# Attention with an adapter: two small transposes move into the free quarters of the score banks, and ahead in TensorE's order

## The chip, the core and the metric

The kernel runs on one core of one Trainium2 chip. The metric is the device time of one execution in microseconds. A profiled execution has a span of its own, from its first to its last instruction, and a time, which is a little longer. PE is TensorE, DVE is VectorE, ACT is ScalarE, POOL is GpSimd, SP is SyncE. PSUM is the memory that PE writes; it has eight banks, each of 512 fp32 columns in 128 partitions.

## The reference, cut to what matters

Four blocks follow one another on x of shape (4, 256, 512): attention with an adapter, a gated FFN, a state-space mixer (most of the time), the gated FFN again. The change is in the first.

```python
B, T, C = x.shape            # 4, 256, 512; 32 heads of 16
qkv = einsum('btc,oc->bto', layernorm(x), w_attn)
q, k, v = split(qkv, 3)      # each (B, 32, T, 16)
q, k = rope(q), rope(k)
scores = where(causal, einsum('bhqd,bhkd->bhqk', q, k) / sqrt(16), -inf)
y = einsum('bhqk,bhkd->bhqd', softmax(scores), v)
# ten adapter tokens: keys ak and values av from w_attn
ascores = gating[0] * softmax(einsum('bhqd,xhkd->bhqk', q, ak) / sqrt(512))
y = y + einsum('bhqk,xhkd->bhqd', ascores, av)
x = x + einsum('btc,oc->bto', y, w_proj)
x = x + ffn(layernorm(x))    # then the mixer, then the FFN again
```

## The kernel before, in words

All of attention is the function `attention`. It has three PSUM pools. `ps` ("a_m") is a ring of three banks for nearly everything: projections (`pq`), turned stacks (`trp`), turned weights (`ptr`), adapter scores (`pa`), and small transposes. `ps_s` ("a_s") has four banks for the scores, each holding 3 x 128 of its 4 x 128 columns. `ps_y` ("a_y") has one for the weighted values `py`.

The prologue prepares batch 0: it splits the weights into upper and lower parts, normalizes x, makes two products each for q and k and two for v (12 matmuls each, `mm3`, lines L115 to L117), and rotates q and k (`rotated`: three DVE instructions from PSUM at L323, L326 and L327, one POOL sum at L329). `stacked` (L342, L343, on POOL) and `pieces` (transposes at L444, a copy at L447, a DMA `pc` on SP's queue) turn them into the form that the scores need. In the prologue a scheduler orders the instructions of every engine.

Then comes a loop of 32 steps: batch b, and u, one of eight groups of four heads. In it PE's order is the program's order (a manual schedule for TensorE alone), while the scheduler orders the other engines. The order of a step i on PE is:

1. the 16 score matmuls of (b, u) at L492; on even steps behind the first `adapter_scores` (`pa`, L457, copied to `sa`, L462); the transposes of `pieces` (L444). DVE reduces the scores in eight instructions (L500), which also write them masked to SBUF; ACT takes exponentials (L508).
2. the "long" item of the step: a product for the next batch's q, k or v (12 matmuls), for an output projection `po`, or for the FFN `pd`; steps 8, 16, 24, 26 and 27 have none. Then "values" items (`pya`).
3. `weigh(i-2)`, 16 matmuls into `py` (L533, L539), which DVE copies to `ys` in `taken` (L547).
4. `turn(i-1)`: 12 transposes into three `ptr` (L523), copied to `eT` by ACT, DVE and ACT (L524).
5. `gathered(i-3)`: two transposes of `ys` into `try` (L553), a DVE reciprocal (L558) and product `y` (L559).
6. the asides: on even steps the second half of `adapter_scores`, two transposes into `tra` (L466) that ACT copies to `as` (L467).
7. "turn" items: `tr` (the normalized x, L166), `pt` (adapter weights, L584), the closing `try2` (L610).

`gathered` and the asides before take a bank each from the three-bank ring, as `ptr` does.

Of the kernel before, what the change touches and what calls it, by code (L numbers as in the profile page):

```python
# [9 lines left out]
F32 = mybir.dt.float32  # L10
# [10 lines left out]
P = 128  # L21
B, L, C = 4, 256, 512
# [4 lines left out]
NH, HD = 32, 16  # L27
# [52 lines left out]
def hybrid_kernel(  # L80
# [18 lines left out]
    a_s = keep.tile([P, 1], F32, name="a_s")  # L99
# [172 lines left out]
    def attention(later, region):  # L272
        with ExitStack() as es:
# [5 lines left out]
            p3 = pool("a3", 3)  # L279
            ps, ps_s, ps_y = (  # L280
                banks.enter_context(tc.tile_pool(name=name, bufs=bufs, space=PSUM))
                for name, bufs in (("a_m", 3), ("a_s", 4), ("a_y", 1))
            )

            acon = w1.tile([P, NCOL_ATTN - NCOL_KEEP], F32, name="acon")
            col = lambda name: acon[:, COLS[name][0] - NCOL_KEEP : COLS[name][1] - NCOL_KEEP]
            rot = col("rot").rearrange("p (c f s d) -> p c f s d", c=2, f=2, s=2)
# [20 lines left out]
                return xs  # L308

            def projected(xs, w, where):  # L310
                pq = where[0].tile([P, C], F32, name="pq", tag=where[1])
                mm3(pq, [[v[:, k, :] for v in xs] for k in range(KC)],
                    [[v[:, k, :] for v in w] for k in range(KC)])
                return pq

            def rotated(pq, c, f, name):

                pv = pq.rearrange("p (h d) -> p h d", h=NH)
                cos, sin = (
                    rot[:, c, f, s, :].unsqueeze(1).to_broadcast([P, NH, HD]) for s in range(2)  # L320
                )
                t1 = p2.tile([P, NH, HD], F32, name="t1", tag="t1")
                nc.vector.tensor_tensor(t1, pv, cos, ALU.mult)  # L323
                t2 = p1.tile([P, NH, HD], F32, name="t2", tag="t2")
                hd = HD // 2
                nc.vector.tensor_tensor(t2[:, :, :hd], pv[:, :, hd:], sin[:, :, :hd], ALU.mult)  # L326
                nc.vector.tensor_tensor(t2[:, :, hd:], pv[:, :, :hd], sin[:, :, hd:], ALU.mult)  # L327
                r = p2.tile([P, NH, HD], F32, name=name, tag=name)
                nc.gpsimd.tensor_tensor(r, t1, t2, ALU.add)  # L329
                return r  # L330
# [23 lines left out]
            AW = 8 * NA  # L354
# [50 lines left out]

            def prepared(b):

                where = (ps, "m") if b else (ps_s, "sc")
                r = {0: -6, 1: 1}.get(b, 8 * (b - 1))
                xs = []  # L410

                def made(c, f):
                    w = wk_s if f else wq_s
                    qk[b, c, f] = rotated(projected(xs[c], w, where), c, f, f"r{f}{c}")

                yield "turn", r
                xs.append(normed(norm, 2 * b))
                yield "long", r + 1
                made(0, 0)
                yield "turn", r + 1  # L420
                xs.append(normed(norm, 2 * b + 1))
                yield "long", r + 2
                made(0, 1)
                yield "long", r + 3
                made(1, 0)
                yield "long", r + 4
                made(1, 1)
                where = (ps, "m")
                for c in range(2):
                    yield "long", r + 5 + c  # L430
                    nc.scalar.copy(
                        values(vs[b % 2], c)[:, :, :HD],
                        projected(xs[c], wv_s, where).rearrange("p (h d) -> p h d", h=NH),
                    )

            def pieces(b, q, f):
# [16 lines left out]
            def adapter_scores(b, q):  # L453
                pa = ps.tile([AW, L], F32, name="pa", tag="m")
                for j in range(4):
                    n = (4 * q + j) * AW
                    nc.tensor.matmul(  # L457
                        pa, akbd[:, n : n + AW], turned_[b, q][0][:, 0, j % 2, :],
                        start=(j == 0), stop=(j == 3),
                    )  # L460
                sa = p2.tile([AW, 4, P], F32, name="sa", tag="paT").rearrange("p s i -> p (s i)")[:, :L]
                nc.scalar.copy(sa, pa)  # L462
                yield
                tr = ps.tile([P, 2, AW], F32, name="tra", tag="m")
                for c in range(2):
                    nc.tensor.transpose(tr[:, c, :], sa[:, c * P : (c + 1) * P], ident[:AW, :AW])  # L466
                nc.scalar.copy(  # L467
                    state[b]["as"][:, :, q * 8 : q * 8 + 8, :].rearrange("p c h a -> p c (h a)"), tr
                )
# [11 lines left out]
            def scores(b, u):  # L481

                qT, kT = turned_[b, u // 2]
                es_ = [p2.tile([P, 4, (c + 1) * P], F32, name=f"e{c}", tag=f"e{c}") for c in range(2)]
                tops = {}
                banks_ = [ps_s.tile([P, 3, P], F32, name="sc", tag="sc") for _ in range(4)]
                for c, at in ((1, slice(0, 2)), (0, slice(2, 3))):
                    n = (c + 1) * P
                    for v in range(2):
                        for r in range(4):  # L490
                            rows = slice(32 * r, 32 * r + 32)
                            nc.tensor.matmul(  # L492
                                banks_[r][:, at, :].rearrange("p k i -> p (k i)"),
                                qT[rows, 0, u % 2, c * P : (c + 1) * P], kT[rows, v, u % 2, :n],
                                start=(v == 0), stop=(v == 1),
                            )
                for c, at in ((1, slice(0, 2)), (0, slice(2, 3))):
                    tops[c] = nm = p3.tile([P, 4], F32, name="nmx", tag="nmx", bufs=4)
                    for r in range(4):
                        nc.vector.tensor_tensor_reduce(  # L500
                            es_[c][:, r, :].rearrange("p (k i) -> p k i", i=P), banks_[r][:, at, :],
                            mask[:, 1 - c :, :], -1.0, 3e38, ALU.add, ALU.min, nm[:, r : r + 1],
                        )

                yield
                for c in (1, 0):
                    for r in range(4):
                        nc.scalar.activation(  # L508
                            es_[c][:, r, :], es_[c][:, r, :], AF.Exp, scale=-1.0, bias=tops[c][:, r : r + 1],
                        )  # L510
                    if c == 0:
                        all_es[8 * b + u] = es_
                    yield
# [34 lines left out]
                return ys  # L548

            def gathered(b, u, ys):  # L550
                tr = ps.tile([P, 2, 4, 32], F32, name="try", tag="m")
                for c in range(2):
                    nc.tensor.transpose(  # L553
                        tr[:, c].rearrange("p h d -> p (h d)"), ys[:, c * P : (c + 1) * P], ident
                    )
                st = state[b]
                ry = p2.tile([P, 2, 4], F32, name="ry")
                nc.vector.reciprocal(ry, tr[:, :, :, HD])  # L558
                nc.vector.tensor_tensor(  # L559
                    st["y"][:, :, 64 * u : 64 * u + 64].rearrange("p c (h d) -> p c h d", h=4),  # L560
                    tr[:, :, :, :HD], ry.unsqueeze(3).to_broadcast([P, 2, 4, HD]), ALU.mult,
                )
# [73 lines left out]
            def fed(f, t):  # L636
# [12 lines left out]
            wq_s, wk_s, wv_s = (  # L649
                [wpool.tile([P, KC, C], F32R, name=f"{v}{j}") for j in range(2)] for v in ("wq", "wk", "wv")  # L650
            )
# [25 lines left out]
            all_es, eTs, yss = {}, {}, {}  # L677
            feed = None
            asides, nexts = [], {}
# [10 lines left out]
            def step(stage, i):  # L690

                for j in [j for j, (s, r) in nexts.items() if s == stage and r <= i]:
                    moved(j, i)
# [15 lines left out]
            with tc.manual_schedule(engines={nc.tensor.engine}):  # L709
                for i in range(n):  # L710
                    b, u = divmod(i, 8)
# [20 lines left out]
                    next(scoring)  # L732
                    step("long", i)
                    step("values", i)
                    if 2 <= i:
                        py = weigh(*divmod(i - 2, 8), eTs.pop(i - 2))
                    if 1 <= i:
# [1 line left out]
                    next(scoring)  # L739
                    if 2 <= i:  # L740
                        yss[i - 2] = taken(py)
                    if 3 <= i:
                        gathered(*divmod(i - 3, 8), yss.pop(i - 3))
                    while asides:
                        next(asides.pop(0), 0)
                    step("turn", i)
                    if u == 7:
                        moved(adapted(b), i)
# [6 lines left out]
                    b, u = divmod(i + 3, 8)  # L755
# [17 lines left out]
                b = B - 1  # L773
# [26 lines left out]
            ps = ctx.enter_context(tc.tile_pool(name="m_m", bufs=2, space=PSUM, **freed))  # L800
# [1111 lines left out]
```

## Time and profile before

| | us |
|---|---|
| three runs | 1806.4, 1806.55, 1808.31 (median 1806.55) |
| profiled execution, its time | 1805.61 |
| its span | 1803.8 |
| mean granted clock of TensorE | 0.989 |
| the loop's first scores | 31.71 |
| PE busy from 135 to 180 us | 42.81 of 45 |
| PE, DVE, ACT, POOL busy over the span | 97%, 79%, 70%, 13% |

The loop of 32 steps and its end take the stretch from 31.71 us to about 290; at about 315 us the mixer is under way and takes nearly all the rest. A step with a long product takes 6.5 to 10 us, one without 4.7 to 8.7. Busy shares are means over stages, so the stretches matter more than the totals. A row of the trace's timeline has the start, the duration, the engine, the line and the tiles; in brackets stands idle time before it and what ended it. Matmuls overlap in the pipeline, so that a row's duration can reach into the next row.

### The profile page before, as it was taken

The page shows a single profiled execution, that of the slowest core. Times are in us where ns is not written, and L with a number is a line of the kernel's source. Part 1 is how long each engine was busy: PE and PEld are TensorE (multiplying, and loading weights), DVE is VectorE, ACT ScalarE, POOL GpSimd, SP SyncE. Part 2 cuts the span into 40 slices and gives each one's busy share as a digit, 9 for nine tenths or more (in the row PEclk, how much of TensorE's full clock was granted, in tenths as well). Part 3 has the DMA queues.
Part 4 walks back from the last instruction along what each step waited for, and adds up shares of the span by engine and source line. Part 5 has one row for each costly group of instructions (what it writes and reads, how often), then busy time and mean ns, then how long its engine had stood idle before and what let it go on. Part 6 is the DMA issues. An engine that isn't in the chain of part 4 may idle for free.

```text
span 1803.8 us, 33220 instructions
## 1 busy us (share of the span) xinstructions
PE 1745.7 (97%) x12862; PEld 1417.8 (79%) x12862; DVE 1427.7 (79%) x2523; ACT 1268.7 (70%) x2293; POOL 240.9 (13%) x249
## 2 busy tenths in 40 slices
PE   7999988899999999999999999999999999999998
PEld 6777767778877888888888888888888888888877
DVE  5676676889998788787878797878788878887777
ACT  5676684578887668766866686668667867777754
POOL 5332320111110111011110101110111101101100
PEclk8999999999999999999999999999999999999999
DMA  4000100122344234423433252325333433343231
GB/s 157 19 19 19 47 26 26 43 71 99 109 127 137 80 106 154 120 85 99 153 100 100 88 162 90 109 81 176 103 94 112 135 106 94 115 138 115 85 97 56
DMA packets 136941, 173.71 MB, mean 96 GB/s; under 512 B 12752, under 2 KB 78032, under 8 KB 136784
## 3 DMA queue, kind: packets, MB, share of 16 engines
q1 hardware_dynamic: 127712, 138.57, 25.5%
q10 hardware_dynamic: 9072, 33.03, 4.8%
q8 instruction: 101, 1.65, 0.4%
q14 instruction: 56, 0.46, 0.1%
HBM read 131.71 MB, written 35.65 MB: 93 GB/s over the span
## 4 chain that ended last, share of the span: by engine, by line
PE 76%; DVE 11%; ACT 8%; issue 3%; DMA 1%; POOL 1%; SPq 0%; ACTq 0%; DVEq 0%; POOLq 0%
PE pp L115 13%; PE pp L117 12%; PE pp L116 12%; PE pyy L1252 7%; PE pog L115 6%; PE pog L117 6%; PE pog L116 6%; PE trx L1233 3%; DVE acc L980 2%; ACT e L508 1%; ACT em L1213 1%; DVE em L1226 1%; PE pq L115 1%; PE ptr L523 1%; PE pq L117 1%
## 5 line engine op out<-in xcount | busy, mean ns | idle before, releaser
L115 PE MATMUL pp<-mx,w 128*128 128x512 f32 x1144 | 459.3, 401 | 0.0
L117 PE MATMUL pp<-mx,w 128*128 128x512 f32 x1144 | 446.8, 391 | 0.0
L116 PE MATMUL pp<-mx,w 128*128 128x512 f32 x1144 | 446.1, 390 | 0.0
L1285 POOL TENSOR_TENSOR sq<-sq,x 128x1024 f32<-128x1024 f32 x54 | 132.1, 2446 | 1177.7 <-ACT x L1284 1177.7
L117 PEld LDWEIGHTS pp<-mx,w 128*128 128x128 f32 x1144 | 214.7, 188 | 46.2
L115 PEld LDWEIGHTS pp<-mx,w 128*128 128x128 f32 x1144 | 214.8, 188 | 44.7
L980 DVE SCALAR_TENSOR_TENSOR acc<-pp,cw_s,acc 128x1012 f32<-128x1012 f32 (+2 forms) x192 | 244.5, 1274 | 4.3
L116 PEld LDWEIGHTS pp<-mx,w 128*128 128x128 f32 x1144 | 215.1, 188 | 40.5
L1226 DVE TENSOR_TENSOR em<-em,gm 128x1280 f32<-128x1280 f32 x128 | 189.5, 1489 | 72.1 <-ACT em L1221 72.1
L115 PE MATMUL pog<-wo,gh 128*128 128x512 f32 x512 | 201.2, 393 | 2.0 <-DVE x L1381 2.0
L117 PE MATMUL pog<-wo,gh 128*128 128x512 f32 x512 | 200.2, 391 | 0.9 <-DVE gh L1364 0.9
L116 PE MATMUL pog<-wo,gh 128*128 128x512 f32 x512 | 199.8, 390 | 0.0
L1236 DVE TENSOR_TENSOR xd<-trx,dt_t 128x512 f32<-128x512 f32 x128 | 82.4, 685 | 141.5 <-PE trx L1233 141.5
L1152 ACT ACT_TABLE_LOAD x63 | 80.8, 1283 | 139.1 <-DVE acc L980 138.9
L1443 ACT ACTIVATE gt<-pp 128x1024 f32<-128x1024 f32 x64 | 65.6, 1025 | 145.0 <-PE pp L117 145.0
L1252 PEld LDWEIGHTS pyy<-em,xd 64*64 64x64 f32 x4096 | 130.2, 133 | 44.2 <-issue 17.6
L1213 ACT ACTIVATE em<-r,end_t 128x128 f32<-128x128 f32 x512 | 163.1, 389 | 0.8
L1252 PE MATMUL pyy<-em,xd 64*64 64x256 f32 (+3 forms) x4096 | 157.8, 300 | 3.1 <-DVE em L1226 3.0
L115 PEld LDWEIGHTS pog<-wo,gh 128*128 128x128 f32 x512 | 96.3, 188 | 24.8 <-issue 2.8
L508 ACT ACTIVATE e<-e,nmx 128x256 f32<-128x256 f32 (+1 forms) x256 | 97.2, 448 | 24.3 <-DVE nmx L500 24.2
L117 PEld LDWEIGHTS pog<-wo,gh 128*128 128x128 f32 x512 | 96.4, 188 | 22.3 <-DVE gh L1364 2.1
L116 PEld LDWEIGHTS pog<-wo,gh 128*128 128x128 f32 x512 | 96.4, 188 | 19.5
(324 smaller groups left out, 3094.5 us busy)
## 6 DMA issues: line engine op xcount, KB each, us to landing
wr<-in_win_dram SPq DMA_DIRECT2D x144, 256.0 KB, 2.7
r<-cumd SPq DMA_DIRECT2D x256, 128.0 KB, 2.9
spill<-gb ACTq DMA_DIRECT2D x63, 512.0 KB, 2.8
gr<-spill SPq DMA_DIRECT2D x120, 256.0 KB, 3.4
wor<-in_wout_dram SPq DMA_DIRECT2D x64, 256.0 KB, 4.4
pc<-pc SPq DMA_DIRECT2D x32, 128.0 KB, 2.0
out_dram<-x SPq DMA_DIRECT2D x7, 256.0 KB, 2.3
x<-in_x_dram SPq DMA_DIRECT2D x1, 1536.0 KB, 9.0
```

The lines of the kernel that those rows point to most:

```text
L115: nc.tensor.matmul(o, lh, rh, start=(first and k == 0), stop=False)
L116: nc.tensor.matmul(o, lh, rl, start=False, stop=False)
L117: nc.tensor.matmul(o, ll, rh, start=False, stop=(last and k == n - 1))
L508: nc.scalar.activation(es_[c][:, r, :], es_[c][:, r, :], AF.Exp, scale=-1.0, bias=tops[c][:, r : r + 1],)
L980: nc.vector.scalar_tensor_tensor(av[:, :, d:], pv[:, :, : L - d], cw_s[:, ch, tap : tap + 1], av[:, :, d:], ALU.mult, ALU.add,)
L1152: nc.scalar.activation(pair(x2).rearrange("p k u i -> p u k i"), acc.rearrange("p (u k i) -> p u k i", u=2, i=Q), AF.Silu,)
L1213: nc.scalar.activation(piece(e, j, c, 2 - c, 2), rv[:, j, 2:, :], AF.Exp, bias=end_t[:, 2 * j + c, h : h + 1],)
L1226: nc.vector.tensor_tensor(e, e, gm, ALU.mult)
L1236: nc.vector.tensor_tensor(xd[:, hs, :].rearrange("p c (h d) -> p c h d", h=2), tr.rearrange("p c (h d) -> p c h d", h=2), dt_t[:, hs, 2 * ...
L1252: nc.tensor.matmul(py[d, u, j * L + c * Q : (j + 1) * L].rearrange("p (k i) -> p k i", i=Q), xd[us, 4 * j + c, d], piece(es2[hh], j, c)[us ...
L1285: (nc.gpsimd if n < NB - 2 else nc.vector).tensor_tensor(sqs[g], sqs[g], x2, ALU.add)
L1443: nc.scalar.activation(gts[i], pp, AF.Silu)
```

## The change

The four score banks become one tile `four` of four banks, 4 x 4 x 128 columns, held for the whole stage. The scores take columns 0 to 383 of each bank as before. `try` goes into the last quarter of the first two banks and `tra` into that of the last two, so neither takes a bank of the ring. Both move ahead in PE's order, from behind `turn` and `taken` to right behind the long and values items, before `weigh`. The four first q/k products of the prologue, which had rotated through the four score buffers, write the four banks of the same tile.

```diff
-                for name, bufs in (("a_m", 3), ("a_s", 4), ("a_y", 1))
+                for name, bufs in (("a_m", 3), ("a_s", 1), ("a_y", 1))
...
+            four = ps_s.tile([P, 4, 4, P], F32, name="sc")
...
             def projected(xs, w, where):
-                pq = where[0].tile([P, C], F32, name="pq", tag=where[1])
+                pq = where if where is not None else ps.tile([P, C], F32, name="pq", tag="m")
...
             def made(c, f):
                 w = wk_s if f else wq_s
+                where = None if b else four[:, 2 * c + f].rearrange("p k i -> p (k i)")
                 qk[b, c, f] = rotated(projected(xs[c], w, where), c, f, f"r{f}{c}")
...
             def adapter_scores(b, q):
...
-                tr = ps.tile([P, 2, AW], F32, name="tra", tag="m")
+                tr = four[:, 2:4, 3, :AW]
...
             def scores(b, u):
...
-                banks_ = [ps_s.tile([P, 3, P], F32, name="sc", tag="sc") for _ in range(4)]
...
-                                banks_[r][:, at, :].rearrange("p k i -> p (k i)"),
+                                four[:, r, at, :].rearrange("p k i -> p (k i)"),
...
             def gathered(b, u, ys):
-                tr = ps.tile([P, 2, 4, 32], F32, name="try", tag="m")
+                tr = four[:, 0:2, 3, :].rearrange("p c (h d) -> p c h d", d=32)
...
                     step("long", i)
                     step("values", i)
+                    if 3 <= i:
+                        gathered(*divmod(i - 3, 8), yss.pop(i - 3))
+                    while asides:
+                        next(asides.pop(0), 0)
                     if 2 <= i:
                         py = weigh(*divmod(i - 2, 8), eTs.pop(i - 2))
                     if 1 <= i:
                         eTs[i - 1] = turn(all_es.pop(i - 1))
                     next(scoring)
                     if 2 <= i:
                         yss[i - 2] = taken(py)
-                    if 3 <= i:
-                        gathered(*divmod(i - 3, 8), yss.pop(i - 3))
-                    while asides:
-                        next(asides.pop(0), 0)
                     step("turn", i)
```

## The prediction

> **What bounds the kernel now.** I read the page's busy shares, then the stretches, then the waits of TensorE in the attention stage. Of the page:
>
> ```profile
> PE 1745.7 (97%) x12862; PEld 1417.8 (79%) x12862; DVE 1427.7 (79%) x2523; ACT 1268.7 (70%) x2293; POOL 240.9 (13%) x249
> ```
>
> PE (TensorE) carries the end. The change touches only the attention stage, which fills the first 315 us; behind it the two programs are the same. Of the stretches of 45 us:
>
> ```profile
> 135.00:180.00 45.00, 42.81 (x393) 33.18 (x391) 30.63 (x133) 31.46 (x79) 12.90 (x27) 1.00 0.05 19
> ...
> 225.00:270.00 45.00, 38.99 (x404) 29.76 (x392) 33.32 (x146) 39.46 (x98) 10.20 (x21) 0.96 0.08 30
> ```
>
> The columns are length, then PE, weight loads, DVE, ACT and POOL busy, clock, DMA. In the middle PE is 95% busy and runs in an order written by hand: a wait put on PE lengthens the span nearly one for one. Only at 225 to 270 is ACT (39.46) as full as PE. What the change can take away stands in PE's waits from 31 to 315 us:
>
> ```profile
> PE try L553 <- ACT eT L524: 5.0, 7, 2.2
> ...
> PE try L553 <- DVE eT L524: 0.4, 1, 0.4
> PE tra L466 <- ACT eT L524: 0.3, 1, 0.3
> ...
> PE tra L466 <- DVE eT L524: 0.2, 1, 0.2
> ```
>
> That is 5.9 us in 10 waits: `try` and `tra` take a slot of the three-buffer ring that `ptr` has just used, and the slot is free only when ptr is copied out to eT. The ring shortage is real, but small. Now an even step with a long product (step 12), on PE and then on DVE (start, duration, instruction):
>
> ```profile
> 137.08 0.40 PE L117 MATMUL pq<-wk,axs 128*128 128x512 f32 x1
> 137.40 0.64 PE L533 MATMUL py<-eT,av 128*32 128x256 f32 x8
> ...
> 138.19 1.53 PE L523 MATMUL ptr<-con,e 128*128 128x128 f32 x12
> 139.58 0.44 PE L553 MATMUL try<-con,ys 128*128 128x128 f32 x2
> 140.07 0.36 PE L466 MATMUL tra<-con,sa 80*128 80x80 f32 x2
> ```
>
> ```profile
> 137.51 0.69 DVE L323 TENSOR_TENSOR t<-pq,acon 128x512 f32<-128x512 f32 x1 [1.36 <-PE pq L117]
> 138.12 0.41 DVE L326 TENSOR_TENSOR t<-pq,acon 128x256 f32<-128x256 f32 x1
> 138.45 0.41 DVE L327 TENSOR_TENSOR t<-pq,acon 128x256 f32<-128x256 f32 x1
> 138.78 0.42 DVE L547 COPY ys<-py 128x256 f32<-128x256 f32 x1
> ...
> 140.05 0.21 DVE L558 RECIPROCAL ry<-try 128x8 f32<-128x8 f32 x1
> 140.30 0.29 DVE L559 TENSOR_TENSOR y<-try,ry 128x128 f32<-128x128 f32 x1
> ```
>
> PE does not wait here. DVE starts the rotation the moment the product ends; the reciprocal and product that read `try` follow far later and nobody waits for them.
>
> **What the change makes of it.** It adds or removes next to no instructions (PE, DVE, ACT and POOL work is the same, so that costs 0); it moves `try` and `tra` up and changes what they wait for. In the changed program as built, all of `four` counts as one tile: an instruction that writes any bank of it waits for readers of every bank. Four new waits follow.
>
> *(a) tra behind the gathering.* The second quarter's transposes (15 even steps) must wait until DVE has read `try` to the end. PE would issue them 0.30 us behind try; DVE needs 0.25 (reciprocal, start to start) + 0.29 (product) and a signal each way of about 0.03 (in the rows above the product ends at 137.48, DVE starts at 137.51): a stall of some 0.55 us at best. But DVE's built order puts other work first. In steps 4, 10, 12, 18 and 20 it is the rotation just shown: from 137.51 DVE needs 0.61 + 0.33 + 0.33 for it, then 0.25 + 0.29, to 139.32; tra could have started at 137.40 + 0.30 = 137.70. With the signal: 1.65 each, 5 x 1.65 = 8.3. In steps 14, 22 and 28 it is the addition of the projected values to x (0.61) and, between reciprocal and product, a statistics instruction (0.65, as the rows of 28 to 34 us have it): again about 1.65, together 5.0. Behind PE stand weigh, ptr and the next scores: all of PE moves. In steps 2, 6 and 30 there is the bare chain or a little more: 0.35 + 0.55 + 1.2 (in 30 DVE's choices of the FFN stand ahead) = 2.1.
>
> *(b) try behind the reductions.* It must wait for the last of the eight score reductions of its step. With a long product (2.8 us) between, they are done. In steps 8, 16, 24, 26 and 27 there is none. Step 8, the end of the reductions on DVE and where try would now be issued on PE:
>
> ```profile
> 103.88 0.28 DVE L500 CUSTOM_DVE_ANT_0 e<-sc,acon 128x128 f32<-128x128 f32 x1
> ```
>
> ```profile
> 102.68 0.64 PE L533 MATMUL py<-eT,av 128*32 128x256 f32 x8
> ```
>
> 104.16 - 102.68 = 1.5 us of wait, and 0.55 for tra; against it go the waits of before in that step (0.31 for try, some 0.8 for what follows). Net 0.8, 0.8, 0.3, 1.3 and 1.2: 4.4 us.
>
> *(c) Smaller ones.* In steps 11 and 19 the product `y` waits for PE's closing transposes and the next scores for it: 0.6 each, 1.2. With try and tra gone from behind ptr, the turn items there meet the ring's copy to eT uncovered (their cover was 0.4 to 0.7 us): 0.3 to 0.4 in 9, 17 and 29, 0.2 in 10, 18 and 28, 0.7 at the end: 2.4.
>
> *(d) What is gained.* Of the 5.9 us, those in steps with (a) and (b) are netted above. What is left is step 23:
>
> ```profile
> 230.10 0.52 PE L553 MATMUL try<-con,ys 128*128 128x128 f32 x2 [2.22 <-ACT eT L524]
> ```
>
> ACT is late there with eT, and py of the next step needs it soon anyway; -1.1. Steps 7, 15 and 25: -0.2, +0.2, -0.3. Together -1.4.
>
> Loop: 8.3 + 5.0 + 2.1 + 4.4 + 1.2 + 2.4 - 1.4 = 22.0. At 225 to 270 ACT is the fuller engine, and part of a PE stall is time PE would have waited for it; I take off half of the 6.8 that fall in steps 24 to 31: -3.4. Loop 18.6.
>
> *(e) The prologue.* The four first q/k products, before in four buffers back to back, now write one tile: each waits for the rotation (reads) of the one before. The turning of the first stack stands ahead of the second q product in PE's new order, and POOL gives that stack here:
>
> ```profile
> 23.39 0.46 POOL L343 TENSOR_TENSOR st<-r,st 128x128 fp32r<-128x128 f32 x1
> ...
> 28.13 1.27 POOL L329 TENSOR_TENSOR r<-t,t 128x512 f32<-128x512 f32 x1
> ```
>
> From 23.85: product 12 x 0.233 = 2.8, rotation 1.35, product 2.8, rotation 1.35, POOL's sum 1.27: 33.4, where before it ended at 29.40. All that follows it hangs on it: +4.0. From below: +2, if PE gets the stack 2 us sooner since POOL's order moved; from above: +8, if PE's clock falls in the gaps (12 products at 0.43, as at 13 to 15 us, cost 2.3 more, twice).
>
> The score banks are read for long: the reductions of step 8 last 2.3 us (101.87 to 104.16). The Trainium skill, "PSUM — Partial Sum Buffer", section "PSUM bank collisions raise a hardware error", says that two engines must not touch one bank and quadrant at once, whatever the columns, so that a free quarter of a bank being read is not free. By that rule (by bank, not by tile) the waits of try in (b) stay, but tra, in other banks than try, need not wait for DVE's product, nor the prologue's products, in four banks, for each other: by the page alone an estimate of about +5 in all. No run here shows a collision; the waits that are built in are what I count.
>
> **Sum.** 1805.6 (profiled run: span 1803.8 and 1.8 outside) + 18.6 + 4.0 = 1828.2. The median of the runs is 0.9 above the profiled one: 1829. A measurement of this kernel can tell about 0.2% (3.6 us) from no change. Unknown costs: (a) is 0.25 to 1.7 per step for 15 steps (4 to 25, taken 15.4, since the rows give DVE's order exactly), prologue 2 to 8, ACT's cover 0 to 7.
>
> **Rivals.**
> 1. *Hidden waits, faster.* If the reads on DVE are over when PE gets there (DVE's short pair ahead of the rotation), the waits of PE cost under 0.1 a step and the ring's relief is kept: 5.9, and the clock that falls behind the gap of 2.22:
>
> ```profile
> 230.00:232.00 2.00, 1.90 (x20) 1.53 (x21) 0.83 (x4) 1.97 (x4) 2.00 (x3) 0.58 0.01 4
> 232.00:234.00 2.00, 2.00 (x24) 1.54 (x22) 2.00 (x16) 1.97 (x4) 2.00 (x5) 0.56 0.00 0
> ```
>
>  4 us at 0.57 are 1.7 lost: 7.6 gained against 4.0 of prologue: 1803. It decides if the new waits are under 3.6 / 15 = 0.24 us a step; the rows say 0.55 at least. 4%.
>
> 2. *Swallowed, no change.* PE waits 24 us in the loop already; if its stalls only replace those (as when ACT bounds every step), the loop stands still and only part of the prologue shows: 1807 to 1810. Against it: from 90 to 225 PE has hardly a gap to give. 5%.
>
> 3. *The clock falls, slower yet.* If gaps of 1.65 pull the clock down as that of 2.22 did (1.7 each, eight of them) or the prologue's do: up to 1842. Against it: gaps of 1.33 and 0.9 (steps 7 and 15) left the clock at 1.00. 11%. The skill's "TensorE: Matmul & The Clock Gate", Part 1, puts the fall behind an idle window of about 3.4 us; by it no new stall would do that, but the row at 230 fell after 2.22.
>
> The forecast holds 80%. Range: 1814 (half of (a) hidden) to 1842 (rival 3). Faster 0.04, within 0.2% 0.05, slower 0.91.
>
> **What would show it.** Right: in PE's waits, lines "tra <- DVE y" with some 15 waits and 14 us, "try <- DVE" on the reductions in five steps, the ring's "try <- ACT eT" gone; scores of step 0 near 35.7 instead of 31.7; the same length from the mixer on. Wrong: tra without waits, or the loop's length (31.7 to 290) up by under 8 us.

## The result, and the profile after

Four runs of the changed kernel took 1833.77 to 1840.81 us, median 1836.45; the kernel before in the same comparison 1807.43. The ratio is 1.0163, with a 95% interval of 1.0142 to 1.0184: 29 us slower. The profiled execution took 1836.36 us, 30.75 more than that of before. Of the page:

```profile
PE 1749.6 (95%) x12862; PEld 1424.4 (78%) x12862; DVE 1428.9 (78%) x2523; ACT 1271.2 (69%) x2293; POOL 241.3 (13%) x249
```

The instructions are as many as before; PE is busy 3.9 us longer with the same matmuls, and stands for some 27 us more. Where, the waits of PE from 38 to 315 us say (in the changed kernel try and tra are parts of the tile `sc`: L552 writes try, L466 writes tra, L491 the scores):

```profile
PE sc L466 <- DVE y L558: 16.6, 12, 2.0
PE sc L552 <- DVE nmx L499: 15.5, 9, 3.8
...
PE sc L466 <- DVE fmv L139: 1.6, 1, 1.6
PE sc L491 <- DVE y L558: 1.1, 3, 0.4
```

Before, no wait of `try`, `tra` or the scores ended with these readers; the ring's 5.9 us are gone. By the starts of the score matmuls, the 30.75 us come about like this: the first scores start at 37.92 instead of 31.71 (+6.2); the steps 0 to 30 last 277.1 instead of 248.8 (+28.3); what follows up to the mixer's first matmul is 3.2 shorter, and the rest 0.6.

*An even step with a rotation.* Step 12 again, PE and then DVE:

```profile
149.03 0.38 PE L552 MATMUL sc<-con,ys 128*128 128x128 f32 x2
151.17 0.33 PE L466 MATMUL sc<-con,sa 80*128 80x80 f32 x2 [1.76 <-DVE y L558]
```

```profile
149.23 0.69 DVE L324 TENSOR_TENSOR t<-pq,acon 128x512 f32<-128x512 f32 x1 [1.47 <-PE pq L117]
...
150.50 0.20 DVE L557 RECIPROCAL ry<-sc 128x8 f32<-128x8 f32 x1
150.73 0.29 DVE L558 TENSOR_TENSOR y<-sc,ry 128x128 f32<-128x128 f32 x1
```

PE has issued try and wants to write tra, two banks away. DVE first rotates, then takes try; PE stands for 1.76 us. The prediction had 1.65.

*A step without a product.* The dearest is step 24, with 12.28 us instead of 7.43. Its try on PE, and DVE ahead of the reductions:

```profile
258.58 0.69 PE L552 MATMUL sc<-con,ys 128*128 128x128 f32 x2 [3.82 <-DVE nmx L499]
```

```profile
255.50 0.18 DVE L144 RECIPROCAL frs<-frs 128x4 f32<-128x4 f32 x1 [1.89 <-ACT frs L143]
255.71 0.59 DVE L158 TENSOR_SCALAR axn<-x,fmv,frs 128x512 f32<-128x512 f32 x1
256.23 0.41 DVE L499 CUSTOM_DVE_ANT_0 e<-sc,acon 128x256 f32<-128x256 f32 x1
```

The reductions (L499) stand behind the normalization of the FFN on DVE, which waits for a square root on ACT, which loads a table first:

```profile
253.87 1.28 ACT L143 ACT_TABLE_LOAD   x1
```

Before, DVE did this behind the reductions, of which this is the first:

```profile
231.70 0.43 DVE L500 CUSTOM_DVE_ANT_0 e<-sc,acon 128x256 f32<-128x256 f32 x1 [0.51 <-PE sc L492]
...
234.69 0.17 DVE L144 RECIPROCAL frs<-frs 128x4 f32<-128x4 f32 x1
```

Then the clock, behind step 16's waits of 1.49 and 0.72 us (the number ahead of the last two is the granted clock, as a share of the full one):

```profile
184.00:186.00 2.00, 2.00 (x23) 1.63 (x20) 0.43 (x1) 0.48 (x3) 0.00 (x0) 0.68 0.04 8
186.00:188.00 2.00, 2.00 (x11) 1.91 (x10) 0.69 (x1) 0.88 (x2) 0.00 (x0) 0.50 0.00 0
```

*The prologue*, last sum of the rotations on POOL, and the last turning on PE:

```profile
31.26 2.52 POOL L108 TENSOR_TENSOR wp<-ar,wp 128x512 fp32r<-128x512 f32 x2
...
34.53 1.26 POOL L330 TENSOR_TENSOR r<-t,t 128x512 f32<-128x512 f32 x1
```

```profile
36.75 0.49 PE L444 MATMUL trp<-con,st 128*128 128x128 f32 x2 [4.68 <-POOL st L344]
```

The four products come one behind the other, and POOL splits the projection's weights ahead of the last sum: it ends at 35.8 where before it ended at 29.4. The size of this varies from one execution to the next: three of the runs below have the same prologue (tra back in the ring, the old order, the spare matmuls), and their first scores start at 37.19, 36.20 and 35.60, that is 3.9 to 5.5 later than before. In the changed kernel's execution the clock stood at 0.50 from 10.64 to 17.47, while the first products ran; in that with 35.60 it stood at 1.00.

### The profile page after: what moved, and what is told of

The parts are those of the page before. It is cut to its first block, busy times and chain, and to the rows that moved or that the text cites. A ratio compares the mean times of both kernels' runs of the same rounds, so it can differ in the third digit from the quotient of the medians.

```text
span 1834.6 us, 33221 instructions
## 1 busy us (share of the span) xinstructions
PE 1749.6 (95%) x12862; PEld 1424.4 (78%) x12862; DVE 1428.9 (78%) x2523; ACT 1271.2 (69%) x2293; POOL 241.3 (13%) x249
## 3 DMA queue, kind: packets, MB, share of 16 engines
q8 instruction: 101, 1.65, 0.4%
## 4 chain that ended last, share of the span: by engine, by line
PE 83%; DVE 9%; ACT 4%; issue 1%; DMA 1%; POOL 1%; SPq 0%; ACTq 0%; DVEq 0%; POOLq 0%
PE pp L115 13%; PE pp L117 13%; PE pp L116 13%; PE pyy L1251 7%; PE pog L115 6%; PE pog L116 6%; PE pog L117 6%; PE trx L1232 3%; PE ptr L522 2%; DVE acc L979 1%; DVE e L499 1%; PE pq L115 1%; PE pq L117 1%; PE pq L116 1%; PE sc L491 1%
## 5 line engine op out<-in xcount | busy, mean ns | idle before, releaser
L919 DVE TENSOR_TENSOR w<-wr,w 128x512 fp32r<-128x512 f32 x138 | 99.5, 726 | 4.4 <-ACT w L916 4.4
```

Source lines behind the costliest of these rows:

```text
L919: nc.vector.tensor_tensor(w[1], r, w[0].bitcast(F32), ALU.subtract)
```

## The experiments

The theory: the time is in waits for readers of other banks of one tile. The rivals: the new order costs it by itself; writing a quarter of a bank that is being read costs it. Ratios are to the kernel before on the same chip, whose median was 1806.8, 1804.9 and 1806.7 us in the three sets of runs.

### The order alone

```diff
 # the kernel before; ring and score banks as they were
                     step("values", i)
+                    if 3 <= i:
+                        gathered(*divmod(i - 3, 8), yss.pop(i - 3))
+                    while asides:
+                        next(asides.pop(0), 0)
...
-                    if 3 <= i:
-                        gathered(*divmod(i - 3, 8), yss.pop(i - 3))
-                    while asides:
-                        next(asides.pop(0), 0)
                     step("turn", i)
```

> The kernel before with only the order moved: gathered and the asides ahead of weigh, but try and tra in the three-bank ring, the score banks as they were. Theory (the waits on the one tile make the time, not the order): no wait of try on the reductions, none of tra on the product y, the prologue as before with the first scores near 31.7 us; the ring gives some small waits of ptr in place of the 5.9 us of try and tra, so 1804 to 1811. Rival (the order itself costs, because weigh, ptr and what hangs on them come later): over half of the 29 us stays, 1822 or more.

Measured 1811.66, ratio 1.0036 (1.0023 to 1.0050): a little beyond the theory's range, but about a fifth of the loss (0.36% of 1.63%), not half. The order does cost something, and the largest part of it in one place: step 24 is 3.66 longer, since tra now waits there for `sa`, which ACT copies only behind its two table loads (steps 7, 8 and 28 are 1.0 to 2.3 longer, step 23 is 2.4 shorter):

```profile
236.72 0.53 PE L466 MATMUL tra<-con,sa 80*128 80x80 f32 x2 [2.72 <-ACT sa L462]
```

### The prologue's products in the ring

```diff
-                    where = None if b else four[:, 2 * c + f].rearrange("p k i -> p (k i)")
+                    where = None
```

> The changed kernel, but the first q and k products of the prologue take banks of the ring, one each. Theory: the first scores come about 6 us sooner than 37.9, near 31.7 to 33, and the loop is as long as in the changed kernel, so about 1830. Rival (what the prologue loses is won back later, as the end of the loop was 3.2 us shorter): within 2 us of 1836.

Measured 1831.38, ratio 1.0149 (1.0124 to 1.0173). The first scores came at 31.07, 6.9 sooner than in the changed kernel; steps 0 to 30 took 278.4, 1.3 more than there. So the loop wins nothing back: the prologue is a cost of its own. How much of it is kept is less sure: the medians are 5 us apart, but the intervals of the two ratios overlap.

### tra back in the ring

```diff
-                tr = four[:, 2:4, 3, :AW]
+                tr = ps.tile([P, 2, AW], F32, name="tra", tag="m")
```

> The changed kernel, but tra takes a bank of the ring, at its new place in the order. Theory: the waits of tra on DVE's product (16.6 us in 12, and 2.3 us beside them) go, those of try on the reductions (about 15.5 us in the loop) and the prologue's 6 us stay: 1815 to 1820. Rival (the wait only moves: ptr or the ring waits for the same DVE work): 1828 or more.

Measured 1812.42, ratio 1.0036 (1.0024 to 1.0048): 24 us less than the changed kernel, by one line, and better than expected. The waits for the product went, as the theory says; those of try on the reductions did not (17.2 us in 9), and the prologue was as in the changed kernel (37.19). In step 12 the loop was 0.35 shorter than before, in step 16 1.07 longer, in 24 and 27 over 4.

### The quarters with the old order

```diff
 # the changed kernel
-                    if 3 <= i:
-                        gathered(*divmod(i - 3, 8), yss.pop(i - 3))
-                    while asides:
-                        next(asides.pop(0), 0)
                     if 2 <= i:
                         py = weigh(*divmod(i - 2, 8), eTs.pop(i - 2))
...
+                    if 3 <= i:
+                        gathered(*divmod(i - 3, 8), yss.pop(i - 3))
+                    while asides:
+                        next(asides.pop(0), 0)
                     step("turn", i)
```

> The changed kernel's one tile with its quarters, but gathered and the asides back behind turn and taken. Theory: try meets reductions long done, so its 15.5 us go; tra still waits for reciprocal and product, about 0.6 us in each of 15 steps (9 us); the ring's 5.9 us are gone; the prologue's 6 us stay: 1814 to 1822. Rival (only the new order meets late readers, at the old place the tile costs nothing but the prologue): 1807 to 1811. Rival (the tile's waits are as dear at the old place): over 1828.

Measured 1823.75, ratio 1.0099 (1.0083 to 1.0116), 2 us over the theory's range. try meets no reductions any more, but the tile has two prices at this place:

```profile
PE sc L466 <- DVE y L558: 10.6, 14, 1.5
PE sc L491 <- DVE y L558: 9.6, 14, 1.8
```

Tra waits for the product in 14 steps, as foreseen; that the next scores wait for it too, in 14 steps, was not.

### The same quarters in two tiles

```diff
-            four = ps_s.tile([P, 4, 4, P], F32, name="sc")
+            four = [ps_s.tile([P, 2, 4, P], F32, name=f"sc{j}") for j in range(2)]
...
-                    where = None if b else four[:, 2 * c + f].rearrange("p k i -> p (k i)")
+                    where = None if b else four[f][:, c].rearrange("p k i -> p (k i)")
...
-                tr = four[:, 2:4, 3, :AW]
+                tr = four[1][:, :, 3, :AW]
...
-                                four[:, r, at, :].rearrange("p k i -> p (k i)"),
+                                four[r // 2][:, r % 2, at, :].rearrange("p k i -> p (k i)"),
...
-                tr = four[:, 0:2, 3, :].rearrange("p c (h d) -> p c h d", d=32)
+                tr = four[0][:, :, 3, :].rearrange("p c (h d) -> p c h d", d=32)
```

(the reductions read `four[r // 2][:, r % 2, at, :]` likewise.)

> The changed kernel with its order and its quarters, but the four banks as two tiles of two banks: try in the quarters of the first pair, tra in those of the second. The banks and columns that are touched stay the same; only what is counted as one tile is halved. Theory (the time is in waits for readers of other banks of one tile): tra's waits on the product y go (19 us), try still waits for six of the eight reductions (about 15 us in the loop), and of the prologue's 6 us about half stays: 1807 to 1813. Rival (writing into a quarter of a bank that is being read costs in itself): over 1825.

Measured 1803.04, ratio 0.9996 (0.9983 to 1.0008). The order and the quarters stay, and the 29 us are gone: so neither the order nor the place of try and tra is the main cost, but what counts as one tile. What it would cost to write a bank while it is read, no run here shows, since the waits prevent it: in the changed kernel's trace no matmul into `sc` starts while DVE or ACT reads that tile. Step 12 of the run with two tiles:

```profile
136.09 0.38 PE L552 MATMUL sc<-con,ys 128*128 128x128 f32 x2
136.31 0.30 PE L466 MATMUL sc<-con,sa 80*128 80x80 f32 x2
```

Tra follows try 0.22 us later, with no wait. The waits of try on the reductions are left, shorter (9.9 us in 9). That the run is some 4 us below the range comes from these, where about 15 us were expected, and from the prologue: its first scores start at 30.17, sooner than before, where half of the loss was expected to stay. The two products of a pair now have another pair's product between them, so that PE waits 0.5 us for a rotation instead of 1.2, and POOL splits the projection's weights behind the last sum, not ahead of it (at 32.79).

### The clock in the waits

```diff
 # the changed kernel
+                    if i in (8, 16, 24, 26, 27):
+                        warmed(ps_y.tile([P, L], F32, name="py", tag="py"), [ones] * 10)
                     step("values", i)
```

> The changed kernel with ten spare matmuls of 128 columns put into the wait ahead of try in steps 8, 16, 24, 26 and 27, where PE stands for 1.5 to 3.8 us. They change no result. Theory (part of the 29 us is the clock that falls to 0.50 after these waits: PE is 3.9 us longer busy with the same matmuls): the clock stays near 1.00 there, and the kernel takes 1 to 4 us less, 1832 to 1835. Rival (the clock falls without a price, or falls all the same): 1836 or a little more.

Measured 1833.41, ratio 1.0159 (1.0139 to 1.0179), against 1.0163 (1.0142 to 1.0184): the medians are 3 us apart as the theory has it, but the intervals overlap, so the total settles nothing. Nor does the profiled execution as a whole: its steps 0 to 30 took 0.9 longer than in the changed kernel, and its first scores came 2.3 sooner. The single steps say more. In 16, 26 and 27 the clock stayed at 1.00 and the steps together took 3.1 us less than in the changed kernel, and 3.0 less than in the run with the prologue's products in the ring, whose loop is the same. In step 24 a wait of 1.53 us was left, the clock fell all the same, and the step took 0.24 less; in step 8, where the clock had not fallen, the spare matmuls cost 0.6. Step 16, first in the changed kernel, then in this run (the ten spare ones stand in the trace as 20):

```profile
184.66 2.80 PE L522 MATMUL ptr<-con,e 128*128 128x128 f32 x12
```

```profile
179.92 2.46 PE L122 MATMUL py<-ones 128*128 128x128 f32 x20
182.22 0.38 PE L552 MATMUL sc<-con,ys 128*128 128x128 f32 x2
...
184.37 1.53 PE L522 MATMUL ptr<-con,e 128*128 128x128 f32 x12
```

So ptr takes 2.80 in the changed kernel and 1.53 here. The spare matmuls last longer (2.3 us) than the wait that they fill (1.49), and yet the step is 0.97 shorter. In steps 10, 23 and 30, where nothing was put in, the clock fell in this run and not in the changed kernel's, and they were 1.3 to 1.6 longer: where no matmuls fill a wait the clock falls in one execution and not in the other.

### The new order only where there is a product

```diff
 # the lines of the order, against the changed kernel
+                    early = any(s == "long" and r <= i for s, r in nexts.values())
                     step("long", i)
                     step("values", i)
-                    if 3 <= i:
-                        gathered(*divmod(i - 3, 8), yss.pop(i - 3))
-                    while asides:
-                        next(asides.pop(0), 0)
+                    for _ in range(early):
+                        if 3 <= i:
+                            gathered(*divmod(i - 3, 8), yss.pop(i - 3))
+                        while asides:
+                            next(asides.pop(0), 0)
...
+                    for _ in range(not early):
+                        if 3 <= i:
+                            gathered(*divmod(i - 3, 8), yss.pop(i - 3))
+                        while asides:
+                            next(asides.pop(0), 0)
                     step("turn", i)
```

In the traces steps 8, 16, 24, 26 and 27 keep the old place, and step 25 too, which has adapter values (`pya`) but no product either.

First with one tile, and the prologue's products and tra in the ring:

> The changed kernel with the prologue's products and tra in the ring, and the new order only in steps that have a long product; in steps 8, 16, 24, 26 and 27 gathered and the asides stand at the old place. Theory: from the 1812.4 of the run with tra in the ring, 5.0 go with the prologue and 10.9 with the five steps (1.06 + 1.07 + 4.05 + 0.51 + 4.24 over before): about 1797, faster than the kernel before. Rival (the gains of the product steps depend on the stalls in the others, or the ring's waits come back): 1804 or more.

Measured 1796.96, ratio 0.9961 (0.9948 to 0.9974): faster than before, at the expected value. Then in two pairs, with the prologue in the ring:

> Two pairs of banks with try and tra in their quarters, the prologue's products in the ring, the new order only in steps with a long product. Theory: as the run by step with the ring, with one user less in the ring: 1794 to 1799. Rival: tra's place in the second pair brings waits of the score reductions on ACT's copy of tra, 1803 or more.

Measured 1797.28, ratio 0.9959 (0.9943 to 0.9974). Then with the prologue in the pairs:

> Two pairs of banks, the new order only in steps with a long product, and the prologue's products in the pairs (in the run with pairs the first scores came at 30.2 us). Theory: as the run with pairs by step, whose prologue in the ring gave first scores at 30.6: 1795 to 1799. Rival (the order of the other engines in the loop shifts with the prologue): off by more than 3 us either way.

Measured 1797.21, ratio 0.9952 (0.9939 to 0.9966). These three can't be told apart. Last without quarters, the kernel before with the order by step:

> The kernel before, its score banks and its ring untouched, with only the new order, and that only in the steps with a long product. Theory (what the quarters give is that try and tra leave the ring to ptr, beside the order): from the 1811.7 of the order alone, the excess in steps 8, 16, 24, 26 and 27 goes (1.01 + 0.57 + 3.66 + 0.97 + 0.51 = 6.7), about 1805, no better than before. Rival (the order by step is the whole gain, the quarters give nothing): 1797 to 1800, as the two runs by step with quarters.

Measured 1801.14, ratio 0.9979 (0.9968 to 0.9991): between the two. By the medians the order by step is worth about half of the gain without any change of memory. That the quarters add the rest is less sure: its interval overlaps those of the first two runs by step and misses that of the third by 0.0002. In the profiled executions their part shows in the rotation steps: 4, 10, 12, 18 and 20 took 0.15 to 0.47 longer than before with the ring, and in the pairs with the prologue in the ring 4 took the same and the others 0.07 to 0.36 less, which is 2.2 of the 3.6 us between these two loops.

## Why the prediction was right, and where its sizes were off

The direction, the mechanism and its lines held: 15.4 us forecast for tra's waits, and the trace has 12 waits for the product with 16.6 us, one for the statistics with 1.6, and two short ones for ACT. 1829 was forecast, 1836.45 measured, in the range of 1814 to 1842. (The lower end is named as half of (a) hidden; half of 15.4 leads to 1821 only, and 1814 needs all of it.) By terms, as the growth of the steps' lengths:

| term | forecast | measured |
|---|---|---|
| rotation steps 4, 10, 12, 18, 20 | 8.3 (and 0.4 of c) | 10.9 |
| steps 14, 22, 28 | 5.0 (and 0.2 of c) | 3.2 |
| steps 2, 6, 30 | 2.1 | 1.1 |
| steps without a product | 4.4 | 14.6 |
| steps 11, 19 | 1.2 | 0.4 |
| steps 9, 17, 29 | 1.1 | -1.1 |
| gains (7, 15, 23, 25) | -1.4 | -1.0 |
| end of the loop | 0.7 | -3.2 |
| cover by ACT | -3.4 | none seen |
| prologue | 4.0 | 6.2 |

That the three rows of (a) come out at 15.2 together, close to the forecast, is in part luck. In steps 4 and 18 the clock fell to 0.50, and they grew by 0.75 and 1.6 more than their like, 12 and 10; without this (a) would be near 12.8.

Term (b) was mis-sized by 10 us. The step that failed is taking step 8 as the pattern of all five. In step 8 it holds (1.07 against 0.8). In 24 the reductions themselves are late, behind a square root's table load; that was to be read from the new order on DVE, since the trace of before has that load in the same step (230.55, 1.28 us) with the reductions ahead of the normalization. In 16, 24, 26 and 27 the clock fell as well: 3.1 us of the term or more, by the spare matmuls in 16, 26 and 27. That was rival 3, given 11%: its mechanism is there, in six steps and not in eight.

The cover by ACT was wrong: I took half of 6.8 us off because ACT was as full as PE at 225 to 270, but the steps 24 to 30 grew by 11.9. PE's dear new waits there are for DVE, and that ACT is full hid nothing that these steps show.

The turn items of steps 9, 17 and 29 did not meet the ring uncovered; the steps became shorter. That comes with the order: with the order alone, and try and tra still in the ring, they were 0.59, 0.60 and 0.32 shorter, and with the quarters at the old place they changed by 0.1 at most. Why the end of the loop became shorter stays open. The clock has a part in it: between the scores of step 31 and the mixer's first matmul it stood at 0.50 for 10.2 us before and for 6.8 in the changed kernel.

The prologue's chain was right as far as the products went (+1.1 us of error on the last rotation, which ended at 33.3); POOL's splitting of the projection's weights and a stack ahead of the last sum were left out; the sum could have started at 33.3 and started at 34.53, 1.2 us later. That is in POOL's new order. In the three other executions of this prologue the term measured 3.9 to 5.5. That 3.9 does not confirm the chain either: the first stack was ready there at 21.8, 2.1 sooner than the 23.85 that the forecast counts from.

The Trainium skill's page "PSUM — Partial Sum Buffer", section "PSUM bank collisions raise a hardware error", asks for guards by bank and quadrant. I had estimated +5 us from it; the two pairs, the nearest to it here, can't be told from before (ratio 0.9996, 0.9983 to 1.0008). The built waits of the changed kernel went further than that rule: they were counted by the tile, and that is the loss. The direction of the counting was taken from the built program, not from the page, and that was the right choice.

## What to carry to other kernels

A free corner of a buffer is free only if nothing else that counts as the same buffer is being read when it is written: ask what the waits are counted by, and cut tiles along the lines of their readers before using the corners. Look at each kind of step by itself: the order that gains up to 0.6 us in a step with a long product costs 0.5 to 4 us in one without, and the mean hides it. Read the new order of every engine that the moved work waits for; a reader that is early in one step can stand behind a table load in another.

## What was not expected of the hardware

The clock does not need a long stand to fall, and like stands end differently. In the changed kernel it fell to 0.50 behind a wait of 1.76 us in steps 4 and 18, and behind waits of 1.49 and 0.72 us with 0.4 us of work between in step 16; behind the same 1.76 us in steps 10 and 12 it stayed at 1.00. In the run with spare matmuls it fell to 0.50 in step 10, where none were put in.

The trace tells these apart. Within one execution the clock's changes lie whole multiples of 3.41 us apart: in the changed kernel it fell at 85.73, 184.72 and 205.20, and rose again 3.41 us after each. Cut the time into windows on that grid, and PE's busy time in one window (the second number) goes with what follows it; these are the windows of steps 10, 12, 16 and 18:

```profile
130.11:133.52 3.41, 2.06 (x10) 1.41 (x9) 2.37 (x15) 2.39 (x8) 0.21 (x2) 1.00 0.00 0
147.18:150.59 3.41, 2.23 (x11) 1.57 (x9) 1.94 (x10) 2.50 (x8) 0.43 (x2) 1.00 0.00 0
181.31:184.72 3.41, 1.55 (x21) 0.88 (x22) 1.59 (x12) 3.02 (x9) 0.92 (x3) 1.00 0.02 5
201.79:205.20 3.41, 1.65 (x16) 1.08 (x18) 2.44 (x6) 1.68 (x6) 1.08 (x1) 1.00 0.00 0
```

Behind the first two the clock stayed, since the edge of a window cuts these waits in two; behind the last two it fell, as it did in step 4 (1.66 busy). In the 12 profiled executions of this case it fell behind all 64 windows at full clock in which PE was busy for less than 0.44 of the time, and behind 5 of some 6050 with 0.60 or more; between the two both happened. So where the grid lies against the kernel decides which of several like waits is caught, and it lies differently in each execution.

Step 16 with and without the spare matmuls gives a price: 0.97 us shorter though 0.63 more was spent ahead of try, so 1.6 us. Steps 8 and 16, both 7.17 us long before, give the same in one execution of the changed kernel: 8.25 where the clock stayed, 9.80 where it fell. For a sum, waits from about 1.5 us up, or two shorter ones close together, carry a chance of that.

The Trainium skill's page "TensorE: Matmul & The Clock Gate", Part 1, puts the fall behind an idle window of about 3.4 us, in a window that runs freely. The length agrees with the grid above, and a window that runs freely agrees with a grid that lies differently in each execution: with the same prologue the clock first fell at 10.64 in the changed kernel and at 33.65 in the run with spare matmuls. That the window must be idle does not agree: PE was busy for 1.55 to 1.66 of the 3.41 us.
